# Stages by batch side by side, places in the same scope, and the second shared expert last

## The chip, the cores and the metric

The kernel runs on one core of one Trainium2 chip. Its time is the device time of one execution in microseconds (us). A core has a matrix engine (TensorE, PE in the profile; its weight loads are listed as PEld), a vector engine (VectorE, DVE), a scalar engine for activation functions and copies (ScalarE, ACT), a general engine (GpSimd, POOL) and one that mostly issues transfers (SyncE, SP). Each works through its own queue of instructions in order; between engines semaphores make one wait for another. Data lie in SBUF (128 partitions), products are formed in PSUM, and DMA queues move data to and from memory (HBM).

## What is computed

The reference takes `x` (4 batches of 512 rows of 512 numbers) through four layers, each an attention-like part and a feed-forward part, every part added to `x` with a gate. Cut to the parts that the change touches:

```python
# L1: attention weights from the context, applied to the rows of ln(x)
x = x + tanh(g_xattn[1]) * L1_xattn(layernorm(x), ctx, Wq, bq, Wk, bk)
# L1: one int8 linear layer, rows quantised one by one
x = x + tanh(g_ffn[1]) * L1_ffn(layernorm(x), weight, w_scale, bias)
# L2: a state-space model over ctx, gated by silu(layernorm(x))
x = x + tanh(g_xattn[2]) * L2_xattn(ctx, layernorm(x), ...)
# L2: 8 experts, the two best of each row, weights made to sum to 1
x = x + tanh(g_ffn[2]) * L2_ffn(layernorm(x), gate_w, w_gate, w_up, w_down)
# L3: attention with rotary positions over ctx
x = x + tanh(g_xattn[3]) * L3_xattn(layernorm(x), ctx, pos, pos, ...)
# L3: 2 shared experts for every row, and the two best of 16 for each row
x = x + tanh(g_ffn[3]) * L3_ffn(layernorm(x), Wsh_up, Wsh_down, Wrt_up, Wrt_down, W_router)
```

## The kernel before

`x` stays in SBUF for the whole kernel, as 16 tiles `x_0` to `x_15` of 128 rows; a batch `b` is four of them (`TB` is 4, `NB` is 4, `NT` is 16). Eight stages, `s0` to `s7`, stand for the eight lines of the reference (the four above that are not L0 are `s2`, `s3`, `s4`, `s5`, `s6`, `s7`). The program text gives the order of the instructions; a scheduler deals them to the engines' queues and may move one ahead inside a scope of higher priority. Tiles come from pools with a fixed number of buffers; a new tile waits until the buffer's last reader is done. A `with net.pools(...)` scope opens the pools of a stage; what comes behind it in the same memory waits for what was there.

Helpers that all stages use: `ln` (statistics on VectorE, L174 and L175; square root on ScalarE, L178; normalised rows `xl`, L205), `lnT` (the same, then 16 transposes on TensorE, L223, and four copies out of PSUM that `evict` deals in turn to VectorE, L162, and ScalarE, L161), `transposed` (four transposes, L234), `chain` (a sum of products on TensorE, L244), `residual` (adds a gated result to a tile of `x` on VectorE, L863).

- `s2`, per batch: two products `pq` with the context make q and k; then for each of four tiles of 128 rows: scores `pe` (L968), the row maximum on VectorE (L973), the exponential on ScalarE (L975), the scaling on VectorE (L977), a transpose into `aT`. Then `lnT` of the batch, four products `po` of four passes each, four residuals.
- `s3`, per batch: `ln`; the row's largest magnitude (L1003), two scalings and a cast on VectorE (L1011, L1014, L1016), a bf16 transpose (L1020), a product of four bf16 passes, then scale, bias and residual on VectorE (L1026, L1030, L863).
- `s4`, per batch: the state output `y` of the batch is loaded, `ln`, Silu on ScalarE (L1227), product with `y` on VectorE (L1229), transposes (L1233), residuals.
- `keys` makes the keys and values of `s6` from the context. It is a generator: `aside(n)` runs n parts of it at the place where it is called, in a scope with a small change of priority. A part has eight passes of `pkv`, the rotation of the keys on VectorE (L1562 to L1564), eight or so transposes (L1586) and two copies on ScalarE (L1655, L1672). In all there are 17 parts.
- `s5`: `top2` has the router (`lnT` of each batch, logits of all 16 tiles in one PSUM tile) and the choice of two experts a row; the normalised rows also go out to memory (`s_xs`) tile by tile. `places` sorts the rows by expert into 39 blocks of 128 rows: `ofi` (the expert of each block) early, the lists `to` and `from` last, behind a sum of 32 passes `inv`. `blocks` then runs over the 39 blocks: `up` reads the block's expert number on SP (`expert`, a value load) and has SP load that expert's weights (L1514 to L1519, 1.9 MB), the block's rows are gathered by an indirect transfer from POOL (L1428), and the results scattered by another (L1455). Results come back to `x` by `combine`: per tile a load `y2` of two times 128 rows and two residuals. `s5`'s results are combined inside `s6`, which isn't touched.
- `s7`: the same with 16 experts and 47 blocks (`rt` weights, 1 MB a block), and two shared experts (`sh0`, `sh1`) that run over all rows: per batch 16 passes `ph`, Gelu on ScalarE (L1990), 16 passes `po`, four residuals. The order in the text is router, places, shared expert 0, shared expert 1, blocks, combine with the write-out of `out` from ScalarE's queue.

The stages are called one after the other, each for all batches, from the driver at the end of the file. There the scopes are: `s2`, `s3`, `s4` and `keys` in one; `s5` whole in the next; `s6`; `s7`.

Of the kernel before, what the change touches and what calls it, by code (L numbers as in the profile page):

```python
# [19 lines left out]
P = 128  # L20
NB = 4
# [27 lines left out]
class Net:  # L49
# [893 lines left out]

    def s2(self, aside):
        nc, a = self.nc, self.a
        wqk = self.w("s2_w")[:, 0 : CC * 256].rearrange("p (c n) -> p c n", c=CC)
        nc.sync.dma_start(wqk, a["s2_w"].rearrange("(c p) n -> p c n", p=P))
        bqk = self.s("s2_b", 2)
        nc.sync.dma_start(bqk, a["s2_b"].rearrange("(k p) -> p k", p=P))
        for b in range(NB):  # L950
            qk = []
            cx = self.context("s2", b)
            for i in range(2):
                pq = self.mm(f"s2_pq_{b}_{i}")
                self.chain(
                    pq,
                    [
                        (wqk[:, c, i * P : (i + 1) * P], cx[:, c, :])
                        for c in range(CC)
                    ],  # L960
                )
                t = self.t(f"s2_qk_{b}_{i}")
                nc.vector.tensor_scalar(t, pq, bqk[:, i : i + 1], None, op0=ALU.add)
                qk.append(t)
            aT = self.w(f"s2_aT_{b}").rearrange("p (k n) -> p k n", k=TB)
            for m in range(TB):
                pe = self.mm(f"s2_pe_{b}_{m}")
                nc.tensor.matmul(  # L968
                    pe, lhsT=qk[0][:, m * P : (m + 1) * P], rhs=qk[1], start=True, stop=True
                )  # L970
                nmx = self.s(f"s2_nmx_{b}_{m}", 1, "s2_nmx")
                sm = self.s(f"s2_sm_{b}_{m}", 1, "s2_sm")
                nc.vector.tensor_reduce(nmx, pe, axis=AX.X, op=ALU.max, negate=True)  # L973
                at = self.t(f"s2_at_{b}_{m}")
                nc.scalar.activation(at, pe, AF.Exp, bias=nmx, accum_out=sm)  # L975
                nc.vector.reciprocal(sm, sm)
                nc.vector.tensor_scalar(at, at, sm, None, op0=ALU.mult)  # L977
# [11 lines left out]
    def s3(self, aside):  # L989
        nc, a = self.nc, self.a  # L990
# [6 lines left out]
        bias = self.bcast("s3_bias", a["s3_bias"])  # L997
        for b in range(NB):
            xl = self.ln(f"s3_{b}", self.x[b * TB : (b + 1) * TB])
            aside(1)  # L1000
            isc = self.s(f"s3_isc_{b}", TB, "s3_isc")
# [7 lines left out]
            for t in range(TB):  # L1009
# [20 lines left out]
                nc.vector.tensor_tensor(h, r, bias, op=ALU.add)  # L1030
                self.residual(b * TB + t, h, self.gf[:, 1:2])


# [182 lines left out]

    def s4(self, aside):
        nc = self.nc
        EC = DC
        for b in range(NB):  # L1220
            aside(1)
# [5 lines left out]
            nc.scalar.activation(g4, g4, AF.Silu)  # L1227
            for e in range(EC):
                nc.vector.tensor_tensor(g[:, e, :], g[:, e, :], y[:, e, :], op=ALU.mult)  # L1229
            for t in range(TB):  # L1230
                pt = self.mm(f"s4_pt_{b}_{t}")
                for e in range(EC):
                    nc.tensor.transpose(  # L1233
                        pt[:, e * P : (e + 1) * P], g[:, e, t * P : (t + 1) * P], self.ident
                    )
                self.residual(b * TB + t, pt, self.gx[:, 2:3])


    def top2(self, name, wr, E, keep=None):


        nc = self.nc
        pr = self.mm(f"{name}_pr")
        for b in range(NB):
            xT = self.lnT(f"{name}_{b}", b, rows=self.sorted[name][1])
            if keep is not None:
                keep.append(xT)
            for t in range(b * TB, (b + 1) * TB):
                self.chain(
                    pr[:, t * E : (t + 1) * E],  # L1250
                    [
                        (xT[:, c, (t % TB) * P : (t % TB + 1) * P], wr[:, c, :])
                        for c in range(DC)
                    ],
                )
        three = lambda v: v.rearrange("p (t e) -> p t e", e=E)
# [8 lines left out]
        m = row("m")  # L1265
        nc.vector.tensor_reduce(m, three(pr[:, 0 : NT * E]), axis=AX.X, op=ALU.max, negate=True)
        nc.vector.tensor_tensor(p, three(pr[:, 0 : NT * E]), wide(m), op=ALU.add)
        nc.scalar.activation(p, p, AF.Exp)
# [25 lines left out]

    def places(self, name, hots, E):

# [7 lines left out]
        tmp = lambda k, n: self.sp.tile([P, n], F32, tag=f"pl_{k}", name=f"{name}_{k}", bufs=1)  # L1304
        room = self.u(f"{name}_room")
        hot, keep, cnt, upto = (room[:, 256 * k : 256 * k + NT * E] for k in range(4))
# [37 lines left out]
        nc.vector.tensor_reduce(of, le, axis=AX.X, op=ALU.add)  # L1344
        ofi = self.sp.tile([P, blocks], I32, tag="pl_ofi", name=f"{name}_ofi", bufs=1)
        nc.vector.tensor_scalar(ofi, of, float(E - 1), None, op0=ALU.min)
# [27 lines left out]
        for i in range(2):  # L1374
# [42 lines left out]
        to, fr = (  # L1417
            self.sp.tile([P, blocks], I32, tag=f"pl_{k}", name=f"{name}_{k}", bufs=1)
            for k in ("to", "from")
        )  # L1420
# [69 lines left out]


    def s5(self):
        nc, a = self.nc, self.a
        E, I = 8, 352
        parts = [(0, P), (P, P), (2 * P, I - 2 * P)]
        wr = self.const.tile([P, DC, E], F32, name="s5_wr")
        nc.sync.dma_start(wr, a["s5_wr"].rearrange("(c p) e -> p c e", p=P))
        hots, tops, m, wide = self.top2("s5", wr, E)
        nc.vector.tensor_tensor(m, tops[0], tops[1], op=ALU.add)
        nc.vector.reciprocal(m, m)  # L1500
        for top in tops:
            nc.vector.tensor_tensor(top, top, m, op=ALU.mult)
        wt = self.gated("s5", hots, tops, m, self.gf[:, 2:3])
        places, ofi = self.places("s5", hots, E)

# [42 lines left out]
        self.blocks("s5", places, up, down)  # L1548
        self.wt5 = wt

# [409 lines left out]
    def s7(self, out):  # L1960
# [4 lines left out]
        xT = []  # L1965
        hots, tops, m, wide = self.top2("s7", wr, ERT, keep=xT)
        wt = self.gated("s7", hots, tops, m, self.gf[:, 3:4])
        places, ofi = self.places("s7", hots, ERT)

# [7 lines left out]

        for e in range(ESH):
            wu, wd = weights(f"sh{e}", a["s7_su"][e : e + 1], a["s7_sd"][e : e + 1])
            for b in range(NB):  # L1980
# [11 lines left out]
                for t in range(TB):  # L1992
                    po = self.mm(f"s7_po_{e}_{b}_{t}")
                    self.chain(
                        po, [(hT[i][:, t * P : (t + 1) * P], wd[:, i, :]) for i in range(2)]
                    )
                    self.residual(b * TB + t, po, self.gf[:, 3:4])

        def up(j, xb):
# [21 lines left out]
        self.blocks("s7", places, up, down)  # L2021
        self.combine("s7", wt, range(NT), out)


@with_exitstack
def kernel(ctx: ExitStack, tc: tile.TileContext, a: dict, out: bass.AP):
# [5 lines left out]
    with net.pools(cp=2, wp=8, up=2, bp=1, tp=8, sp=2, gp=1, qp=3, ps1=4, psb=1):  # L2032
# [10 lines left out]
        for _ in states:  # L2043
            pass
    with net.pools(cp=2, kp=1, rp=1, wp=8, bp=2, tp=10, sp=2, ps2=2, ps1=4):
        keys = net.keys()

        def aside(n):
            with tc.high_priority(offset=-400):
                for _ in range(n):  # L2050
                    next(keys, None)
# [12 lines left out]
    with net.pools(op=1, wp=6, bp=1, up=6, tp=8, sp=2, ps2=2, ps1=4):  # L2064
        net.s7(out)
# [83 lines left out]
```

## Time and profile before

| what | us |
|---|---|
| three runs, median (lowest to highest) | 3263.85 (3263.54 to 3266.96) |
| the profiled execution | 3266.79 |
| its span, first to last instruction | 3264.8 |
| TensorE busy in the span | 2816.4 (86%) |
| VectorE busy | 1953.6 (60%) |
| ScalarE busy | 1197.6 (37%) |
| mean granted TensorE clock | 0.922 of full speed |
| first product of `s2` to the last logit of `s5`'s router | 1450.4 to 1811.96 |
| last logit to the first product of `s5`'s blocks | 1811.96 to 1847.39 |
| shared expert 1 | 2980.2 to 3034.9 |
| blocks of `s7` | 3034.9 to 3226.2 |
| combine of `s7` | 3226.2 to 3264.8 |

A row of a table of stretches reads: the stretch, its length, then for PE, PEld, DVE, ACT and POOL the busy time with the number of instructions, the granted TensorE clock, the share of the 16 DMA engines that is busy, and what they move in GB/s. In the forty slices a digit is a busy share in tenths; in the chain of waits each line is a start, a length, an engine and the line of the kernel, each released by the one above. A transfer's line in a timeline shows when it is issued, not when it lands.

### The profile page before, as it was taken

Reading aid. Unit: us, or ns where it says so; the run is one execution under the profiler, and the core shown is the slowest. Engines: PE = TensorE matmul, PEld = TensorE weight load, DVE = VectorE, ACT = ScalarE, POOL = GpSimd, SP = SyncE. Lnnn points to the kernel's source line nnn. Section 1 sums busy time; section 2 is a strip of 40 time slices with the busy share of each in tenths; the row PEclk is TensorE's granted clock in tenths of the full one; section 3 lists DMA queues with packets and bytes.
Section 4 is the critical chain, followed back from the end, with each engine's and each line's share of the span. In section 5 each row is a group of like instructions: output and inputs, shape, how many; then the busy total and the mean of one; then the engine's idle time right before and its main releaser. Section 6 shows DMA issues by size and latency. Waiting matters only on the chain.

```text
span 3264.8 us, 43075 instructions
## 1 busy us (share of the span) xinstructions
PE 2816.4 (86%) x15772; PEld 1436.1 (44%) x15776; DVE 1953.6 (60%) x3212; ACT 1197.6 (37%) x2061; POOL 977.9 (30%) x939
## 2 busy tenths in 40 slices
PE   6899897878998898988836699977999999989994
PEld 2333332234444444444414588852333333254673
DVE  6565755477988879965687311138666666544103
ACT  2343442365554444433222111113555555520231
POOL 3465664435655646740000122210000000000351
PEclk8899998878999989999967699987999999989997
DMA  4000000266876768851212599972000000022798
GB/s 131 7 1 8 1 1 1 86 233 191 242 212 183 234 187 239 240 153 60 79 59 89 191 321 326 326 260 86 14 28 14 28 1 1 1 78 81 284 384 315
DMA packets 266898, 438.76 MB, mean 134 GB/s; under 512 B 32400, under 2 KB 114576, under 8 KB 265152
## 3 DMA queue, kind: packets, MB, share of 16 engines
q1 hardware_dynamic: 250624, 386.72, 37.0%
q0 software_dynamic: 13760, 45.10, 3.8%
q10 hardware_dynamic: 2304, 4.20, 0.3%
q8 instruction: 126, 2.06, 0.3%
q14 instruction: 84, 0.69, 0.1%
HBM read 370.79 MB, written 65.13 MB: 134 GB/s over the span
## 4 chain that ended last, share of the span: by engine, by line
PE 36%; DVE 8%; issue 4%; ACT 3%; POOL 2%; DMA 2%; POOLq 0%; DVEq 0%; ACTq 0%
PE s_po L244 9%; PE s_pl L268 8%; PE pg_s L244 6%; ACT pr_s L1939 2%; PE s_pq L244 2%; PE s_av L268 2%; PE s_ph L244 2%; POOL s_ys L1455 1%; DMA s_y<-s_ys 1%; DVE x L863 1%; POOL s_xb L1428 1%; PE s_pr L244 1%; PE s_pkv L244 1%; PE pt_s L223 1%; DVE st_s L174 1%
## 5 line engine op out<-in xcount | busy, mean ns | idle before, releaser
L1146 POOL TENSOR_TENSOR s_h<-s_h,s_C 128x512 f32<-128x512 f32 x256 | 449.2, 1754 | 292.1 <-DVE s_h L1145 249.8
L268 PE MATMUL s_pl<-s_qT,s_kT 32*128 32x512 f32 (+1 forms) x1536 | 447.4, 658 | 60.5 <-ACT pr_s L846 23.6
L268 PE MATMUL s_ps<-s_kT,s_qT 32*128 32x512 f32 (+1 forms) x1536 | 441.2, 677 | 12.7 <-DVE s_top L1819 5.9
L1819 DVE TENSOR_REDUCE s_top<-s_ps 128x1 f32<-128x512 f32 x512 | 328.5, 685 | 108.6 <-PE s_ps L268 108.4
L1939 ACT ACTIVATE pr_s<-s_pl 128x512 f32<-128x512 f32 x512 | 278.0, 595 | 307.2 <-PE s_ps L268 297.5
L1145 DVE TENSOR_TENSOR_SCAN s_h<-s_da,s_db 128x512 f32<-128x512 f32 x256 | 312.1, 1219 | 62.6 <-PE s_y L268 36.1
L1144 ACT ACTIVATE s_da<-s_rdl,s_A 128x512 f32<-128x512 f32 x256 | 184.4, 722 | 331.5 <-DVE s_h L1145 329.4
L268 PE MATMUL s_av<-pr_s,s_v 128*32 128x256 f32 (+1 forms) x3072 | 250.8, 398 | 0.2
L244 PE MATMUL s_ph<-xT_s,s_wu 128*128 128x256 f32 x1024 | 246.4, 395 | 0.7 <-ACT xT_s L161 0.7
L905 PE MATMUL s_acc<-s_wd,s_hT 128*128 128x512 f32 x512 | 239.9, 612 | 5.7 <-ACT s_hT L936 5.7
L244 PEld LDWEIGHTS s_ph<-xT_s,s_wu 128*128 128x128 f32 x1024 | 197.3, 197 | 77.9 <-issue 49.7
L244 PEld LDWEIGHTS pg_s<-s_xbT,s_w 128*128 128x128 f32 (+1 forms) x1872 | 213.9, 183 | 19.8 <-issue 17.8
L268 PEld LDWEIGHTS s_pl<-s_qT,s_kT 32*128 32x128 f32 (+1 forms) x1536 | 118.4, 186 | 226.8 <-ACT pr_s L1939 95.9
L244 PE MATMUL pg_s<-s_xbT,s_w 128*128 128x128 f32 (+1 forms) x1872 | 215.5, 275 | 1.4 <-ACT s_xbT L161 1.4
L694 DVE TENSOR_REDUCE s_nmx<-s_ps 128x1 f32<-128x496 f32 x256 | 158.4, 662 | 91.8 <-PE s_ps L268 81.0
L1143 DVE TENSOR_TENSOR s_db<-s_B,s_rdu 128x512 f32<-128x512 f32 x256 | 203.6, 795 | 12.7 <-DMA s_B<-s_bc 5.0
L1332 POOL IOTA s_js<- 128x39 f32 (+1 forms) x2 | 0.4, 178 | 686.8 <-DVE x L863 686.8
L1428 POOL DMA_INDIRECT s_xb<-s_xs,s_from x86 | 83.5, 971 | 380.0 <-PE ptr_s_xb L234 235.2
L846 ACT ACTIVATE pr_s<-s_pl 128x512 f32<-128x512 f32 (+1 forms) x256 | 138.8, 594 | 158.6 <-PE s_pl L268 83.8
L268 PE MATMUL s_y<-s_h,ident 64*64 64x512 f32 x1024 | 146.8, 637 | 53.1 <-issue 28.6
L268 PEld LDWEIGHTS s_av<-pr_s,s_v 128*32 128x32 f32 (+1 forms) x3072 | 61.4, 109 | 285.7 <-issue 253.6
L1534 DVE TENSOR_TENSOR g_s<-g_s,pg_s 128x256 f32<-128x256 f32 x78 | 27.5, 352 | 264.2 <-ACT g_s L1533 264.2
(388 smaller groups left out, 4453.8 us busy)
## 6 DMA issues: line engine op xcount, KB each, us to landing
s_B<-s_bc SPq DMA_DIRECT2D x256, 256.0 KB, 5.0
s_C<-s_bc SPq DMA_DIRECT2D x256, 256.0 KB, 4.4
s_w<-in_s_wg SPq DMA_DIRECT2D x39, 704.0 KB, 4.7
s_w<-in_s_wu SPq DMA_DIRECT2D x39, 704.0 KB, 6.7
s_w_rt<-in_s_ru SPq DMA_DIRECT2D x47, 512.0 KB, 10.8
s_w_rt<-in_s_rd SPq DMA_DIRECT2D x47, 512.0 KB, 12.1
s_w<-in_s_wd SPq DMA_DIRECT2D x39, 512.0 KB, 8.2
s_y<-s_ys SPq DMA_DIRECT2D x32, 512.0 KB, 5.7
```

The source lines that it names most:

```text
L244: ins = self.nc.tensor.matmul(out, lhsT=l, rhs=r, start=(i == 0), stop=(i == len(pairs) - 1)).ins
L268: ins = self.nc.tensor.matmul(out, lhsT=l, rhs=r, **flags).ins
L694: ins = nc.vector.tensor_reduce(nmx[:, at + i : at + i + 1], ps[i][0][:, 0:M], axis=AX.X, op=ALU.max, negate=True,).ins
L846: ins = nc.scalar.activation(prs[i][0:n, j, :], pl[j][0][0:n, :], AF.Exp).ins
L905: ins = nc.tensor.matmul(accs[i][t], lhsT=hT[:, j, t * P : (t + 1) * P], rhs=wd[f // 4][:, f % 4, :], start=(f == 0), stop=(f == FC - 1),).ins
L1143: nc.vector.tensor_tensor(db, br, du, op=ALU.mult)
L1144: nc.scalar.activation(da, dl, AF.Exp, scale=am[:, e, n : n + 1])
L1145: nc.vector.tensor_tensor_scan(h, da, db, 0.0, op0=ALU.mult, op1=ALU.add)
L1146: nc.gpsimd.tensor_tensor(h, h, cr, op=ALU.mult)
L1428: self.nc.gpsimd.indirect_dma_start(out=t, out_offset=None, in_=self.sorted[name][1], in_offset=bass.IndirectOffsetOnAxis(ap=fr[:, j : j + ...
L1819: ins = nc.vector.tensor_reduce(dst[:, i], ps[i][0], axis=AX.X, op=ALU.max, negate=True).ins
L1939: ins = nc.scalar.activation(prs[i][:, j, :], pl[j][0], AF.Exp).ins
```

## The change

`s2`, `s3` and `s4` no longer loop over the batches; each loads its weights and returns `batch(b)`, a generator that stops (`yield`) at places inside the batch: in `s2` after q and k, after every second tile, after `lnT` and after every second product; in `s3` after the norm and after each tile; in `s4` after the Silu and after every second tile. The router is taken out of `top2` and returned the same way, with one PSUM tile per batch, from which ScalarE copies the logits to an SBUF tile `lg`. The driver runs seven steps; in a step, batch `step - i` of stage i is run for each of the four stages, one piece of each in turn, and every second turn one part of `keys`. The scope takes one pool more (`op`, from `places`) and 12 instead of 10 buffers for `t`. `s5_places` (`top2` and `places`) follows in the same scope, its working tile from the pool `w` instead of `u`; `lg`, `ofi`, `to` and `from` lie in an outer pool `hp`. The blocks of `s5` get a scope of their own. In `s7` shared expert 1 is run behind the blocks, batch by batch, with the combine of the batch before it after each; y2 has 6 buffers instead of 4.

```diff
-    def s2(self, aside):
+    def s2(self):
...
-        for b in range(NB):
+        def batch(b):
...
                 qk.append(t)
+            yield
...
                 self.transposed(f"s2_{b}_{m}", at, aT[:, :, m * P : (m + 1) * P], m)
+                if m % 2:
+                    yield
             xT = self.lnT(f"s2_{b}", b, room=self.w)
-            aside(2)
+            yield
             for t in range(TB):
...
                 self.residual(b * TB + t, po, self.gx[:, 1:2])
+                if t % 2:
+                    yield
+        return batch
...
-    def top2(self, name, wr, E, keep=None):
+    def router(self, name, wr, E, room=None, keep=None):
+        lg = self.hp.tile([P, NT * E], F32, name=f"{name}_lg")
+        def batch(b):
+            xT = self.lnT(f"{name}_{b}", b, rows=self.sorted[name][1], room=room)
             if keep is not None:
                 keep.append(xT)
+            yield
+            pr = self.mm(f"{name}_pr_{b}")[:, 0 : TB * E]
+            for t in range(TB):
                 self.chain(
                     pr[:, t * E : (t + 1) * E],
+                    [(xT[:, c, t * P : (t + 1) * P], wr[:, c, :]) for c in range(DC)],
+                )
+            self.nc.scalar.copy(lg[:, b * TB * E : (b + 1) * TB * E], pr)
+        return lg, batch
...
+    def s5_places(self):
+        nc = self.nc
+        hots, tops, m, wide = self.top2("s5", self.lg5, 8)
...
+        self.wt5 = self.gated("s5", hots, tops, m, self.gf[:, 2:3])
+        self.places5 = self.places("s5", hots, 8, self.w)
...
-        for e in range(ESH):
+        def shared(e):
...
+                yield
+        for e in range(ESH - 1):
+            for _ in shared(e):
+                pass
...
         self.blocks("s7", places, up, down)
-        self.combine("s7", wt, range(NT), out)
+        done = lambda b: self.combine("s7", wt, range(b * TB, (b + 1) * TB), out)
+        for b, _ in enumerate(shared(ESH - 1)):
+            if b:
+                done(b - 1)
+        done(NB - 1)
...
-        net.s2(aside)
-        net.s3(aside)
-        net.s4(aside)
-        for _ in keys:
-            pass
+    with net.pools(hp=1):
+        with net.pools(op=1, cp=2, kp=1, rp=1, wp=8, bp=2, tp=12, sp=2, ps2=2, ps1=4):
...
+            stages = [net.s2(), net.s3(), net.s4(), net.s5_router()]
+            turns = 0
+            for step in range(NB + len(stages) - 1):
+                going = [f(step - i) for i, f in enumerate(stages) if 0 <= step - i < NB]
+                while going:
+                    going = [g for g in going if next(g, going) is None]
+                    turns += 1
+                    if turns % 2:
+                        aside(1)
+            for _ in keys:
+                pass
+            net.s5_places()
+        with net.pools(ep=4, bp=1, tp=8, ps2=2, ps1=4):
+            net.s5()
     net.y2 = 2
-    with net.pools(op=1, ep=4, bp=1, up=3, tp=8, sp=2, ps2=2, ps1=4):
-        net.s5()
...
-    net.y2 = 4
-    with net.pools(op=1, wp=6, bp=1, up=6, tp=8, sp=2, ps2=2, ps1=4):
+    net.y2 = 6
+    with net.pools(hp=1, op=1, wp=6, bp=1, up=6, tp=8, sp=2, ps2=2, ps1=4):
         net.s7(out)
```

More of the change, by code (lines that the diff above doesn't have):

```diff
@@ L986, in s2, with s3 @@
                 self.residual(b * TB + t, po, self.gx[:, 1:2])
-    def s3(self, aside):
+                if t % 2:
+                    yield
+        return batch
+    def s3(self):
         nc, a = self.nc, self.a
@@ L997, in s3 @@
         bias = self.bcast("s3_bias", a["s3_bias"])
-        for b in range(NB):
+        def batch(b):
             xl = self.ln(f"s3_{b}", self.x[b * TB : (b + 1) * TB])
-            aside(1)
+            yield
             isc = self.s(f"s3_isc_{b}", TB, "s3_isc")
@@ L1031, in s3 @@
                 self.residual(b * TB + t, h, self.gf[:, 1:2])
+                yield
+        return batch
     def states(self):
@@ L1215, in states, with s4, batch @@
         channels_done(*done)()
-    def s4(self, aside):
+    def s4(self):
         nc = self.nc
         EC = DC
-        for b in range(NB):
-            aside(1)
+        def batch(b):
             y = self.w(f"s4_y4_{b}").rearrange("p (c n) -> p c n", c=EC)
@@ L1227, in s4 @@
             nc.scalar.activation(g4, g4, AF.Silu)
+            yield
             for e in range(EC):
@@ L1236, in s4, with batch, top2 @@
                 self.residual(b * TB + t, pt, self.gx[:, 2:3])
-    def top2(self, name, wr, E, keep=None):
[L1242 to L1245, printed above, removed]
+                if t % 2:
+                    yield
+        return batch
+    def router(self, name, wr, E, room=None, keep=None):
+        lg = self.hp.tile([P, NT * E], F32, name=f"{name}_lg")
+        def batch(b):
+            xT = self.lnT(f"{name}_{b}", b, rows=self.sorted[name][1], room=room)
             if keep is not None:
                 keep.append(xT)
-            for t in range(b * TB, (b + 1) * TB):
+            yield
+            pr = self.mm(f"{name}_pr_{b}")[:, 0 : TB * E]
+            for t in range(TB):
                 self.chain(
                     pr[:, t * E : (t + 1) * E],
[L1251 to L1254, printed above, removed]
-                )
+                    [(xT[:, c, t * P : (t + 1) * P], wr[:, c, :]) for c in range(DC)],
+                )
+            self.nc.scalar.copy(lg[:, b * TB * E : (b + 1) * TB * E], pr)
+        return lg, batch
+    def top2(self, name, lg, E):
+        nc = self.nc
         three = lambda v: v.rearrange("p (t e) -> p t e", e=E)
@@ L1265, in top2 @@
         m = row("m")
-        nc.vector.tensor_reduce(m, three(pr[:, 0 : NT * E]), axis=AX.X, op=ALU.max, negate=True)
-        nc.vector.tensor_tensor(p, three(pr[:, 0 : NT * E]), wide(m), op=ALU.add)
+        nc.vector.tensor_reduce(m, three(lg), axis=AX.X, op=ALU.max, negate=True)
+        nc.vector.tensor_tensor(p, three(lg), wide(m), op=ALU.add)
         nc.scalar.activation(p, p, AF.Exp)
@@ L1292, in gated, with places @@
         return tops
-    def places(self, name, hots, E):
+    def places(self, name, hots, E, room):
         nc = self.nc
@@ L1304, in places @@
         tmp = lambda k, n: self.sp.tile([P, n], F32, tag=f"pl_{k}", name=f"{name}_{k}", bufs=1)
-        room = self.u(f"{name}_room")
+        room = room(f"{name}_room")
         hot, keep, cnt, upto = (room[:, 256 * k : 256 * k + NT * E] for k in range(4))
@@ L1344, in places @@
         nc.vector.tensor_reduce(of, le, axis=AX.X, op=ALU.add)
-        ofi = self.sp.tile([P, blocks], I32, tag="pl_ofi", name=f"{name}_ofi", bufs=1)
+        ofi = self.hp.tile([P, blocks], I32, name=f"{name}_ofi")
         nc.vector.tensor_scalar(ofi, of, float(E - 1), None, op0=ALU.min)
@@ L1417, in places @@
         to, fr = (
-            self.sp.tile([P, blocks], I32, tag=f"pl_{k}", name=f"{name}_{k}", bufs=1)
-            for k in ("to", "from")
+            self.hp.tile([P, blocks], I32, name=f"{name}_{k}") for k in ("to", "from")
         )
@@ L1489, in combine, with s5_router @@
                 self.nc.scalar.dma_start(out[t * P : (t + 1) * P, :], self.x[t])
+    def s5_router(self):
+        wr = self.const.tile([P, DC, 8], F32, name="s5_wr")
+        self.nc.sync.dma_start(wr, self.a["s5_wr"].rearrange("(c p) e -> p c e", p=P))
+        self.lg5, batch = self.router("s5", wr, 8, self.w)
+        return batch
+    def s5_places(self):
+        nc = self.nc
+        hots, tops, m, wide = self.top2("s5", self.lg5, 8)
+        nc.vector.tensor_tensor(m, tops[0], tops[1], op=ALU.add)
+        nc.vector.reciprocal(m, m)
+        for top in tops:
+            nc.vector.tensor_tensor(top, top, m, op=ALU.mult)
+        self.wt5 = self.gated("s5", hots, tops, m, self.gf[:, 2:3])
+        self.places5 = self.places("s5", hots, 8, self.w)
     def s5(self):
@@ L1495, in s5 @@
         parts = [(0, P), (P, P), (2 * P, I - 2 * P)]
[L1496 to L1504, printed above, removed]
+        places, ofi = self.places5
         def up(j, xT):
@@ L1548, in s5 @@
         self.blocks("s5", places, up, down)
-        self.wt5 = wt
     def rope(self, name, ps, t, out):
@@ L1965, in s7 @@
         xT = []
-        hots, tops, m, wide = self.top2("s7", wr, ERT, keep=xT)
+        lg, batch = self.router("s7", wr, ERT, keep=xT)
+        for b in range(NB):
+            for _ in batch(b):
+                pass
+        hots, tops, m, wide = self.top2("s7", lg, ERT)
         wt = self.gated("s7", hots, tops, m, self.gf[:, 3:4])
-        places, ofi = self.places("s7", hots, ERT)
+        places, ofi = self.places("s7", hots, ERT, self.u)
         def weights(name, up, dn):
@@ L1997, in s7 @@
                     self.residual(b * TB + t, po, self.gf[:, 3:4])
+                yield
+        for e in range(ESH - 1):
+            for _ in shared(e):
+                pass
         def up(j, xb):
@@ L2044, with aside @@
             pass
[L2045 to L2051, printed above, removed]
-        net.s2(aside)
-        net.s3(aside)
-        net.s4(aside)
-        for _ in keys:
-            pass
+    with net.pools(hp=1):
+        with net.pools(op=1, cp=2, kp=1, rp=1, wp=8, bp=2, tp=12, sp=2, ps2=2, ps1=4):
+            keys = net.keys()
+            def aside(n):
+                with tc.high_priority(offset=-400):
+                    for _ in range(n):
+                        next(keys, None)
+            stages = [net.s2(), net.s3(), net.s4(), net.s5_router()]
[8 more added lines that the diff above has]
+            for _ in keys:
+                pass
+            net.s5_places()
+        with net.pools(ep=4, bp=1, tp=8, ps2=2, ps1=4):
+            net.s5()
     net.y2 = 2
-    with net.pools(op=1, ep=4, bp=1, up=3, tp=8, sp=2, ps2=2, ps1=4):
-        net.s5()
     with net.pools(wp=2, kq=4, vp=2, up=1, rp=1, tp=8, bp=1, sp=2, ps3=4, ps1=1):
         net.s6()
-    net.y2 = 4
-    with net.pools(op=1, wp=6, bp=1, up=6, tp=8, sp=2, ps2=2, ps1=4):
+    net.y2 = 6
+    with net.pools(hp=1, op=1, wp=6, bp=1, up=6, tp=8, sp=2, ps2=2, ps1=4):
         net.s7(out)
```

## The prediction

> **What bounds the kernel now.** I read the forty slices first, for where the stages lie and who is full in them; then the chain of waits, for what each stage waits for; then busy time by stretch, whose rows are the terms of the sum; then groups by shape, for single durations. The slices (82 us each):
>
> ```profile
> PE   6899897878998898988836699977999999989994
> DVE  6565755477988879965687311138666666544103
> PEclk8899998878999989999967699987999999989997
> DMA  4000000266876768851212599972000000022798
> ```
>
> The change touches slices 18 to 22 (TensorE falls to 3, 6, 6; its clock to 6 and 7) and the last four. The stretches, with the times between which I take each stage:
>
> ```profile
> core 0: us, PE busy (x) PEld busy (x) DVE busy (x) ACT busy (x) POOL busy (x), PEclk, DMA share, GB/s
> 1492.60:1530.70 38.10, 33.66 (x114) 17.04 (x113) 20.94 (x47) 11.44 (x19) 0.00 (x0) 1.00 0.21 70
> ...
> 1667.30:1704.60 37.30, 13.46 (x47) 6.16 (x48) 34.66 (x83) 12.33 (x12) 0.00 (x0) 0.60 0.16 51
> ...
> 1776.60:1811.96 35.36, 33.69 (x192) 32.04 (x190) 15.93 (x38) 7.49 (x12) 0.32 (x2) 0.63 0.43 155
> 1811.96:1847.39 35.43, 5.80 (x41) 4.74 (x41) 20.12 (x60) 0.93 (x3) 5.38 (x6) 0.50 0.68 230
> 2980.20:3034.90 54.70, 53.95 (x127) 23.18 (x126) 12.01 (x16) 4.34 (x8) 0.00 (x0) 1.00 0.06 19
> 3034.90:3226.20 191.30, 185.97 (x1129) 139.87 (x1126) 17.36 (x25) 58.77 (x117) 87.22 (x89) 1.00 0.98 353
> 3226.20:3264.80 38.60, 0.00 (x0) 0.00 (x0) 23.79 (x32) 0.00 (x0) 0.00 (x0) 0.50 0.89 326
> ```
>
> These rows are one s2 batch (TensorE-bound), one s3 batch (VectorE 34.66 of 37.30, TensorE a third), s5's router, s5's places, and at the end shared expert 1, the 47 blocks and the combine. Shared expert 1 has TensorE full and the DMA queues at 0.06; the combine has TensorE at nothing and the queues at 0.89. The chain shows what an s2 tile hangs on:
>
> ```profile
> 1507.19 0.88 PE s_pe L968 x2
> 1508.09 0.70 DVE s_nmx L973
> 1508.81 0.79 ACT s_at L975 x2
> 1509.82 0.50 DVE s_at L977
> 1510.36 0.66 PE ptr_s L234 x4
> ```
>
> It passes from TensorE to VectorE, ScalarE, VectorE and back, 3.5 to 4 us a tile, with nothing else in the four queues. Whoever puts other work into them lengthens it.
>
> **The tail (s7).** Shared expert 1 is moved from before the blocks to behind them. All its instructions go along, in the emitted order: TensorE runs shared expert 0, 47 blocks, then shared expert 1; its products are not mixed into the blocks. So the blocks begin 54.7 us earlier, and their last product, which ended at 3222.4, ends at 3167.7. Behind it stand four batches of 16 and 16 passes, 6.87 + 7.02 = 13.9 by the chain's rows, 55.6, plus 0.9 for the last Gelu, which nothing follows: 3224.2. The combine's 16 loads of 512 KB (38.6 us with the write-out) now run below those 56 us: the queues carried 19 GB/s there, and loading is behind the last scatter (2.7 us) just as before. VectorE has four residuals and eight combine steps a batch, 12 x 0.75 = 9, below TensorE's 13.9. After the last product three VectorE steps (2.3) and the write-out (3.75 between the last VectorE step, 3261.05, and the end) remain: end 3230.3 instead of 3264.8, **34 won**. Queues passed: SP now issues five routed experts' loads ahead instead of four, and shared expert 1's only when block 41 frees its buffer, some 20 us before they are needed; ScalarE issues the write-outs ahead of the next Gelu, with y2 buffers raised from 4 to 6. Bounds: 28, if every write-out holds the next batch's Gelu by 2 us; 36.
>
> **s2 to the router.** Before, 1450.4 to 1811.96, 361.6 us. By batch, summed from the groups' mean durations at full clock (TensorE, VectorE): s2 24.9 and 16.4; s3 6.6 and 21; s4 3.5 and 9.6; router 8.4 and 6; one of 17 parts of the keys 4.3 and 2.25. After, step 0 is s2 alone, step 1 s2 and s3, step 2 with s4, step 3 all four, steps 4 to 6 run out; keys fall at 3.5 parts a step, gone by step 4. The larger engine per step is then 42 (as the first batch took), 46.5 (TensorE), 55, 61, 43 (VectorE), and 25 and 14 for the last two, where one batch hangs on its own chain: 287. That is the lower bound, 75 won.
>
> What it leaves out: the in-order queues. I followed the emitted order with single durations. In step 1, an s2 tile's maximum, exponential and scaling stand between s3's quantising steps: 59. In step 2 the first exponential stands on ScalarE behind the square roots and the Silu of s3's and s4's norms, which themselves wait for VectorE: it comes 24 us into the step instead of 6, TensorE is empty from 12 to 25, and the step takes 70. In step 3 the fourth batch's q and k are evicted by VectorE behind s4's and the router's norms (16.4), its first scores come at 21: 83. Steps 4 to 6: s3's last batch, its own chain with s4's and the router's work between, 56; then 25 and 14. Sum 42 + 59 + 70 + 83 + 95 = 349. Not in it: the low clock in the holes and waits for PSUM and tile buffers. The same four products of s3 took 1.05 at clock 1.0 and 1.90 in the 0.6 stretches; the steps have three holes of about 12 and the last two run thin: 8. Buffers (four PSUM tiles for four stages, 12 tile buffers that s5's row writes free only on landing): 3. **360, 2 won**. Worst: 380 to 386, if each of 12 exponentials in steps 1 to 3 waits 2 us beyond this.
>
> On the clock the row is: 0.60 with TensorE at 13.46 of 37.30, 1.00 at 33.66 of 38.10. The Trainium skill, "TensorE: Matmul & The Clock Gate", Part 1, says that half rate follows an idle window of about 3.4 us and full rate a busy one of as long. By that, three holes of 12 us cost an estimated 3 x 1.7 = 5 for the rewarming; the sum would be 3 lower. The rule speaks against a stretch that is interleaved but has holes, and the trace agrees in direction.
>
> **Between router and blocks.** Before, logits end 1811.96, the first block's product starts 1847.39. Router logits are now copied from PSUM by ScalarE: one 128x32 copy on the path, 0.35 (512 columns take 0.59); in s7 0.5, half hidden by shared expert 0. Blocks now have pools of their own, opened behind the places' pools: in the order of SP's queue 31 reads of the block's expert number stand ahead of the first weight load, before one. Price of one:
>
> ```profile
> 1824.98 0.62 SPq L1519 DMA_DIRECT2D s_w<-in_s_wd  x1
> 1826.40 0.38 SPq L1514 DMA_DIRECT2D s_w<-in_s_wg  x1
> ```
>
> Between these two lie a read and a gap: 0.80; the gap between loads of one expert is 0.19, so 0.61 a read. 31 take 18.9 behind ofi (10.2 after the logits): the first load is issued at 29 after the logits, before at 11.3. It takes about 7 to land, and the rows of the first block, fetched through POOL behind inv, arrive at 34 and gate the first product as before. Only the later loads are late: three buffers filled by 1847 before; now 1.92 MB a block at 325 GB/s, 5.9, against 8.33 TensorE needs a block. Loss 3; bounds 0 and 10. At the stretch's head s6_wkv is loaded behind s1's last product, up to 1; s2_w gates there anyway.
>
> **Sum.** 3264.8 - 34 - 2 + 3 + 0.6 = 3232.4 as a span. The profiled execution took 3266.8 as a whole, 2.0 above its span and 2.9 above the median of 3263.85; 3232.4 + 2.0 - 2.9 = 3231.5, and I say **3230**.
>
> **Rivals.** (B) The stretch overlaps nearly as the busy times allow: the waits I put at 62 above 287 fall to 20 to 30. For it: VectorE holds 245 of 361.6, TensorE 254, much of it at low clock, the router's 33.69 at 0.63. Against: s2's chain through all four queues. 3231 - 45 = 3186 (3165 to 3212). (C) Slower: ScalarE's queue holds s2's exponentials behind other stages' roots, Silus and 1.28 us table loads, tile for tile: 12 tiles in steps 1 to 3 at 4 to 6 us beyond my walk, 48 to 72, with the clock low throughout; the 34 is eaten from about 2.9 us a tile on: 3272. Against: half of those tiles come after the norms of their step. (D) The combine isn't hidden: write-outs in ScalarE's queue or y2 buffers let it run behind the shared expert; 38.6 stays, 3265. Against: queues at 0.06 below it. (E) The interleave does nothing, since the scheduler keeps stage order; the emitted order speaks against it, and it would give 3231 too.
>
> **Chances.** Forecast 0.54 (3214 to 3250), B 0.29, C 0.10, D 0.04, the rest 0.03. About 0.2%, 6.5 us, is what can be told from no change. Range 3174 to 3256: it holds the forecast and most of B. Faster: forecast, B and part of the rest, 0.85; same 0.05; slower 0.10.
>
> **What would show it.** TensorE full and y2 loads landing in the last 56 us, end some 6 us behind the last product: the tail. The time from the first pq to the last logit: 360, else B (below 335) or C (above 395); in step 2 a hole of about 12 before the second scores, released by ScalarE. The first wg issue 29 after the last logit and blocks 8.33 apart from the fourth on. I am wrong if the stretch differs by more than 15, or if the weights' late start costs more than the rows' arrival hides.

## The result and the profile after

| | us |
|---|---|
| before, median (lowest to highest) | 3263.69 (3261.83 to 3266.96), four runs |
| changed, median (lowest to highest) | 3212.78 (3208.02 to 3218.71), four runs |
| ratio, with its 95% interval | 0.9844 (0.9822 to 0.9865) |
| predicted | 3230 (3174 to 3256) |
| the profiled execution of the changed kernel and its span | 3208.97, 3207.3 |

The changed kernel is 51 us faster. The forecast was 34; the difference lies in one stretch. The forty slices of the changed kernel, 80 us each:

```profile
PE   6899898768988989998776599987999999989999
DVE  6665666378897979976777411118666666735004
PEclk8899999878999989999897699997999999989999
DMA  4000000177676767862222499964000000013996
```

From slice 19 on TensorE reads 8, 7, 7, 6, 5 where it read 8, 8, 3, 6, 6; at the end it reads 9 to the last slice where it ended in a 4, and the DMA queues end in 3, 9, 9, 6 where they ended in 2, 7, 9, 8. The stretches, in the columns of the table of before:

```profile
core 0: us, PE busy (x) PEld busy (x) DVE busy (x) ACT busy (x) POOL busy (x), PEclk, DMA share, GB/s
1447.31:1786.03 338.72, 252.46 (x958) 144.34 (x958) 247.91 (x570) 93.22 (x140) 0.84 (x3) 0.85 0.23 75
1786.03:1821.12 35.09, 5.77 (x40) 4.75 (x41) 20.12 (x60) 3.65 (x5) 6.38 (x7) 0.50 0.16 52
1821.12:2149.35 328.23, 327.55 (x2258) 270.88 (x2258) 40.62 (x97) 55.29 (x135) 69.69 (x72) 0.99 0.94 314
2962.50:3143.95 181.45, 180.94 (x1087) 135.35 (x1086) 15.92 (x23) 56.97 (x114) 84.20 (x86) 1.00 1.02 367
3143.95:3207.30 63.35, 55.49 (x129) 23.64 (x127) 34.24 (x49) 4.34 (x8) 1.13 (x2) 0.98 0.61 207
```

The rows are: first product of `s2` to the last logit; from there to the first product of the blocks; the 39 blocks; the 47 blocks of `s7`; from their last product to the end. The first of them, in the profile of the kernel before, was:

```profile
1450.43:1811.94 361.51, 253.89 (x948) 145.87 (x952) 244.83 (x567) 93.08 (x137) 0.32 (x2) 0.81 0.21 71
```

Busy times are the same within 3.1 us (TensorE 253.89 and 252.46, VectorE 244.83 and 247.91); the length fell by 22.8. Nothing was made cheaper; TensorE's idle time went from 107.6 to 86.3.

With both profiles cut at the same events, the 57.5 us between the two spans come out like this (changed less before, us, each time rounded):

| stretch | before | changed | difference |
|---|---|---|---|
| start to `s1`'s last product (code untouched) | 1443.8 | 1439.9 | -3.9 |
| to `s2`'s first product | 6.7 | 7.4 | +0.8 |
| to the router's last logit | 361.5 | 338.7 | -22.8 |
| to the first product of `s5`'s blocks | 35.5 | 35.1 | -0.4 |
| 39 blocks | 327.4 | 328.2 | +0.8 |
| to the first `pb` product of `s7`'s blocks | 866.9 | 813.1 | -53.8 |
| 47 blocks | 180.8 | 181.4 | +0.6 |
| to the end | 42.4 | 63.3 | +20.9 |

The first row is chance: over the twelve profiles of this study `s1` ended between 1434.2 and 1444.3, with the same instructions of TensorE, VectorE and ScalarE ahead of it; E4 below, the changed kernel once more, has the 1434.2.

### The profile page after: what moved, and what is told of

It is laid out like the page before. It is cut to its first block, busy times and chain, and to the rows that moved or that the text cites. A ratio compares the mean times of both kernels' runs of the same rounds, so it can differ in the third digit from the quotient of the medians.

```text
span 3207.3 us, 43093 instructions
## 1 busy us (share of the span) xinstructions
PE 2814.8 (88%) x15776; PEld 1434.8 (45%) x15776; DVE 1952.4 (61%) x3212; ACT 1200.9 (37%) x2071; POOL 976.3 (30%) x939
## 5 line engine op out<-in xcount | busy, mean ns | idle before, releaser
L1157 ACT ACTIVATE s_da<-s_rdl,s_A 128x512 f32<-128x512 f32 x256 | 184.4, 722 | 328.2 <-DVE s_h L1158 324.7
```

The costliest lines, as they stand in the source:

```text
L1157: nc.scalar.activation(da, dl, AF.Exp, scale=am[:, e, n : n + 1])
```

## The experiments

**The parts alone.** E1 to E4 ran side by side on one chip. E1 is the kernel before with the order of `s7` changed and nothing else:

```diff
-        for e in range(ESH):
+        for e in range(ESH - 1):
+            for _ in shared(e):
+                pass
...
-        self.combine("s7", wt, range(NT), out)
+        done = lambda b: self.combine("s7", wt, range(b * TB, (b + 1) * TB), out)
+        for b, _ in enumerate(shared(ESH - 1)):
+            if b:
+                done(b - 1)
+        done(NB - 1)
...
-    net.y2 = 4
+    net.y2 = 6
```

Expected:

> The kernel before with shared expert 1 and the combine moved behind s7's blocks, nothing else. Theory (the tail is worth the 54.7 us of the shared expert less about 21 us that the end grows by): 34 us faster, 3228 to 3232, and the end comes 62 to 63 us after the last block's product. Rival (the tail is worth more, and the stretch little): 45 us or more, below 3220. Rival (the write-outs or the y2 loads hold the shared expert): under 28 us, above 3236.

Measured: 3228.01 against 3261.45 (ratio 0.9897, 0.988 to 0.9913), 33.4 us faster, and the end comes 63.0 us after the last block's product. The theory holds, its rivals fall.

E2 is the changed kernel with `s7` as it was (the diff above, undone):

> The changed kernel with s7 in its old order (shared expert 1 before the blocks, combine alone at the end, 4 buffers for y2). Theory (the interleaved stretch takes 339 us instead of 361.6): 17 to 23 us faster than the kernel before, 3241 to 3247. Rival (the stretch is even, as forecast, and the rest of the difference in the profile is chance of one execution): 3258 to 3264.

Measured: 3252.52 (3239.44 to 3259.16, ten runs), 8.9 us faster (ratio 0.9971, 0.9957 to 0.9984). Neither expectation. In its profile the stretch is 344.3, 17 below the 361.5 of the first profile of before, but it is only 12 below E1's 356.1, where the stretch has before's code; and from `s5`'s last product to `s6`'s first it took 30.2 us instead of 26.7. So the expectation rested on one profile of before that was a long one, and something behind the blocks takes part of the gain back; E7 finds it.

E3 keeps the changed kernel's scopes, pools and tail, and runs the batches stage by stage:

```diff
-            for step in range(NB + len(stages) - 1):
-                going = [f(step - i) for i, f in enumerate(stages) if 0 <= step - i < NB]
-                while going:
...
+            for i, f in enumerate(stages):
+                for b in range(NB):
+                    if i == 2:
+                        aside(1)
...
+                    for k, _ in enumerate(f(b)):
+                        if i == 0 and k == 3:
+                            aside(2)
+                        if i == 1 and k == 0:
+                            aside(1)
```

> The changed kernel with its scopes, pools and tail, but the batches run stage by stage and the keys at the places of before. Theory (the interleave itself makes the gain of the stretch): the stretch from the first pq to the last logit goes back to 358 to 364 us and the time to 3228 to 3236. Rival (the new pools make it: 12 tile buffers, places in the same scope, the router's room): within 5 us of the changed kernel, 3208 to 3218.

Measured: 3232.18 (3229.05 to 3233.32; ratio 0.9913, 0.9896 to 0.9929). Its stretch:

```profile
1443.84:1800.93 357.09, 250.91 (x958) 141.45 (x958) 246.15 (x570) 93.44 (x140) 0.84 (x3) 0.82 0.22 71
```

357.09 us with the same 251 of TensorE and 246 of VectorE: the interleave makes the gain, not the pools.

E4 is the changed kernel again:

> The changed kernel once more, for a second profile and for its spread (3208 to 3219 over four runs). Theory (the spread comes from the TensorE clock in the stretch, which has holes): a time near 3217 goes with a stretch near 348 and a lower granted clock there, one near 3208 with 339. Rival (it comes from s0 and s1, whose end lay 3.9 us apart between the two profiles): the stretch is 339 in both, and the difference lies ahead of it.

Measured: 3214.82 (3210.28 to 3220.84; ratio 0.9863, 0.9842 to 0.9884), the profiled execution 3211.58, with `s1` ending at 1434.2 and a stretch of 342.9. Both theories say too little: against the first profile the stretch is 4.2 longer and `s1` 5.7 shorter. No execution near 3217 was profiled, so what makes those stays open; one source is shown below.

These four give the parts from medians of runs taken together: the tail -33.4 (E1 against before), the new scopes +4.2 (E3 against E1), the interleave -17.4 (E4 against E3); together -46.6, which is E4 against before. Scopes and interleave are -13.2 in this sum and -8.9 in E2, which has them without the new tail; the ten runs of E2 lie 20 us apart, and what spreads them stays open.

**Where the interleave loses.** The changed kernel, per step, against the walk of the prediction (steps 4 to 6, behind `s2`'s last product, are called the drain; it is cut at `s3`'s last product):

| | step 0 | 1 | 2 | 3 | `s3`'s last batch | rest | sum |
|---|---|---|---|---|---|---|---|
| walked | 42 | 59 | 70 | 83 | 56 | 39 | 349 |
| changed | 42.2 | 60.0 | 71.2 | 77.2 | 52.7 | 35.3 | 338.7 |
| E2 | 41.9 | 60.3 | 71.3 | 82.9 | 52.9 | 35.1 | 344.3 |
| E4 | 42.6 | 61.2 | 71.2 | 79.8 | 52.8 | 35.3 | 342.9 |

Step 2 has the hole that was walked, 9.2 us instead of 12 to 13. ScalarE's queue and TensorE's in the changed kernel (start, duration, engine, line, operation, and in brackets what the engine waited for):

```profile
1557.21 0.30 ACT L178 ACTIVATE rs_s<-mv_s,eps 128x4 f32<-128x4 f32 x1 [2.84 <-DVE mv_s L175]
...
1560.93 1.91 ACT L1240 ACTIVATE s_g<-s_g 128x2048 f32<-128x2048 f32 x1
...
1569.12 0.30 ACT L178 ACTIVATE rs_s<-mv_s,eps 128x4 f32<-128x4 f32 x1 [4.98 <-DVE mv_s L175]
1569.44 1.28 ACT L978 ACT_TABLE_LOAD   x1
1570.73 0.69 ACT L978 ACTIVATE s_at<-s_pe,s_nmx 128x512 f32<-128x512 f32 x1
```

```profile
1559.67 3.70 PE L244 MATMUL s_pkv<-s_wkv,ctx_s 128*128 128x512 f32 x8 [1.17 <-ACT s_kt L1703]
1572.57 0.47 PE L1617 MATMUL pt_s6k<-ident,s_k_r 128*128 128x128 f32 x1 [9.20 <-ACT s_vs L1686]
1572.96 1.11 PE L234 MATMUL ptr_s<-ident,s_at 128*128 128x128 f32 x4
```

The first exponential of the step (L978) starts at 1570.73, 21.2 us into it, behind the square roots of the other stages' norms (L178) and the Silu (L1240); TensorE ends its products of the keys at 1563.4 and stands for 9.2 us. The releaser is named as a copy of the keys (`s_vs`), which ScalarE ran right behind that exponential: one queue holds both. E5 lets `s2` run ahead in each step:

```diff
                 going = [f(step - i) for i, f in enumerate(stages) if 0 <= step - i < NB]
+                if step < NB:
+                    next(going[0])
+                    next(going[0])
                 while going:
```

> The changed kernel, where in each of the first four steps s2's batch runs its first two pieces (q and k, two tiles) before the other stages begin. Theory (the holes of steps 2 and 3 come from s2's exponentials standing in ScalarE's queue behind the other stages' square roots and Silu): the hole of 9.2 us in step 2 and most of three holes of 3.4 to 4.6 in step 3 go, steps 2 and 3 shrink from 71 and 80 to about 62 and 72, the stretch from 342 to about 325, the time to 3197 to 3203. Rival (VectorE's work in its queue is what limits; putting s2 first makes the other stages late by as much): the stretch stays at 336 to 348.

Measured: 3218.59 (3211.94 to 3222.35; ratio 0.9879, 0.9861 to 0.9896), no gain, and the stretch is 339.7, as the rival has it. But the steps were 48.8, 66.4, 69.0, 64.9 and then 90.5: steps 2 and 3 shrank, as the theory has it, and steps 0 and 1 together grew by 11 to 13 us. So E9 has the lead in steps 2 and 3 alone, on the kernel of E7 below:

```diff
+                if step in (2, 3):
+                    next(going[0])
+                    next(going[0])
```

> The kernel of the pool kept open for s6, where s2's batch runs its first two pieces ahead of the other stages in steps 2 and 3 only. With the lead in all four steps, steps 2 and 3 took 69.0 and 64.9 instead of 71.2 and 77 to 83, and steps 0 and 1 48.8 and 66.4 instead of 42 and 60. Theory (a lead helps where the exponentials stood behind the square roots and the Silu of s4 and the router, which begin in steps 2 and 3, and harms where s2 has only its own chain and the keys to fill it): steps 42, 60, 69, 65, then 90; the stretch 326, the time 3196 to 3203. Rival (what the lead wins in steps 2 and 3 is work that steps 0 and 1 had done earlier, VectorE's above all): steps 2 and 3 come back to 145 or more in sum, the stretch 338 to 344.

Measured: 3199.77 (3199.26 to 3201.87; ratio 0.9805, 0.9789 to 0.9821). Its steps, the last three in one row:

```profile
1451.91:1493.90 41.99, 37.59 (x110) 19.03 (x111) 26.52 (x68) 12.68 (x22) 0.00 (x0) 0.95 0.20 62
1493.90:1552.90 59.00, 48.94 (x181) 24.66 (x182) 45.51 (x104) 15.81 (x26) 0.00 (x0) 1.00 0.23 72
1552.90:1616.40 63.50, 49.83 (x175) 26.27 (x176) 52.42 (x120) 24.00 (x32) 0.00 (x0) 0.84 0.22 68
1616.40:1685.46 69.06, 50.62 (x197) 30.18 (x198) 52.73 (x119) 22.30 (x32) 0.00 (x0) 0.83 0.27 85
1685.46:1780.73 95.27, 60.01 (x295) 42.14 (x293) 69.94 (x159) 23.42 (x32) 0.32 (x2) 0.73 0.26 87
```

42.0, 59.0, 63.5, 69.1, 95.3: the sum is 328.8 where 326 was expected; steps 2 and 3 lost 18 us against E4 (71.2 and 79.8), and the drain took 7 back (95.3 against 88.1). The edit also moves work: the two pieces ahead count no turns, so 16 products of the keys (two parts) leave step 3 for the drain, and one part's work on VectorE leaves step 2. The net gain is what counts, 9.7 us of the stretch against E7 (338.5) and 14.1 against E4. In ScalarE's queue the exponentials (L978) now stand between the roots and the Silu:

```profile
1556.02 0.30 ACT L178 ACTIVATE rs_s<-mv_s,eps 128x4 f32<-128x4 f32 x1 [3.23 <-DVE mv_s L175]
...
1560.64 0.69 ACT L978 ACTIVATE s_at<-s_pe,s_nmx 128x512 f32<-128x512 f32 x1
...
1562.73 0.30 ACT L178 ACTIVATE rs_s<-mv_s,eps 128x4 f32<-128x4 f32 x1
...
1565.25 0.69 ACT L978 ACTIVATE s_at<-s_pe,s_nmx 128x512 f32<-128x512 f32 x1
...
1567.35 1.91 ACT L1240 ACTIVATE s_g<-s_g 128x2048 f32<-128x2048 f32 x1
```

The first starts at 1560.64, 7.7 us into the step. Four table loads of 1.28 us more are paid for it in this step, and still it is 7.7 us shorter, with as many products of the keys in it (24) as in the changed kernel. The queue's order held the exponentials, not ScalarE's load; how much of step 3's gain is the order and how much the moved keys, no run separates. This kernel beats both: it is 64 us under before, where the changed kernel is 47 to 51 under and E7 48 (each against runs of before beside it; E9 and E10 ran on another chip than E1 to E8).

E10 gives the lead to step 4 too, where `s3`'s last batch comes first:

> The same with the lead in step 4 too, where s3's last batch is the first in turn. Theory (the drain hangs on s3's last batch; let ahead of s4 and the router it ends earlier): steps 4 to 6 from 88 to 90 down to 82, 6 to 8 us faster than with the lead in steps 2 and 3. Rival (VectorE does the work of all three in any order, and the last router batch waits for the same sum): no change within 3 us.

Measured: 3201.73 (3198.88 to 3205.12; ratio 0.9815, 0.9798 to 0.9831); the drain 94.3 against 95.3. The rival holds: no change.

E6 takes the keys out of step 0 (`if turns % 2 and step:`):

> The changed kernel, where no part of the keys runs in step 0; the parts that it had there run in steps 4 and 5. Theory (the last three steps, 88 us with TensorE idle for over a third, have room; step 0 is TensorE-bound with keys): step 0 from 42 to about 34, steps 4 to 6 from 88 to about 90, the stretch 336. Rival (step 0 is bound by the chain of its tiles, and the keys lie in its gaps): step 0 stays at 39 to 42, and steps 4 to 6 grow by VectorE's 2.25 us a part, 7 to 9 in sum: slower, 349.

Measured: 3223.23 (3218.98 to 3225.14; ratio 0.9885, 0.9867 to 0.9903), by the median slower than E4, though the intervals overlap. Step 0 and the drain:

```profile
1451.52:1493.60 42.08, 36.05 (x96) 17.50 (x97) 18.33 (x36) 8.32 (x15) 0.00 (x0) 0.90 0.09 29
1700.09:1794.56 94.47, 66.26 (x295) 45.57 (x294) 66.80 (x157) 25.64 (x34) 0.32 (x2) 0.76 0.28 93
```

The edit did half of what it says: 16 products of the keys (22 in the changed kernel) still moved ahead into step 0, so that TensorE's share of the theory was hardly tested, and what left it is their work on VectorE, 8 us (18.33 against 26.52 in E9's row). Step 0 takes 42.08 all the same: that work cost nothing there. The drain grew from 88.1 to 94.5, and a part of the keys now runs behind the last logit, so that the first product of the blocks comes 38.3 us after it instead of 35.1. In this the rival holds; the whole stretch, 343.0, is as long as E4's, where 349 was expected.

**Between the stages.** E8 puts `s5_places` back into the scope of the blocks, so that one read of an expert number, not 31, stands ahead of the first weight load:

```diff
-            net.s5_places()
-        with net.pools(ep=4, bp=1, tp=8, ps2=2, ps1=4):
+        with net.pools(op=1, ep=4, bp=1, up=1, tp=8, sp=2, ps2=2, ps1=4):
+            net.s5_places()
             net.s5()
```

> The changed kernel, where s5_places stands in the scope of the blocks as before, so that one read of an expert number instead of 31 stands ahead of the first weight load on SP. Theory (the rows of the first block gate it, and the late weights cost only what the first product waits for them, 3.1 us in the profile, less what the blocks lose later, 0.8): first weight load about 12 us after the last logit instead of 29, first product 34 to 35 us after it as before, 39 blocks in 327.4 instead of 328.3: 0 to 2 us faster. Rival (the rows are late too, because the weights share the queues with them): first product up to 5 us earlier, or later.

Measured: 3212.8 (3205.42 to 3220.16; ratio 0.985, 0.9831 to 0.9868). The first weight load on SP's queue in the changed kernel (last logit 1786.03), then in E8 (last logit 1791.87):

```profile
1815.48 0.43 SPq L1546 DMA_DIRECT2D s_w<-in_s_wg  x1
```

```profile
1803.98 0.42 SPq L1546 DMA_DIRECT2D s_w<-in_s_wg  x1
```

29.4 us after the logits there, 12.1 here; the first product stands 35.1 and 35.9 after them, and the 39 blocks take 328.2 and 328.7. What the first product (`pg`, behind the transposes `ptr_s_xb` of the block's rows) waits for is not the same in the two. The changed kernel, then E8:

```profile
1816.90 1.09 PE L234 MATMUL ptr_s_xb<-ident,s_xb 128*128 128x128 f32 x4 [5.67 <-DMA s_xb<-s_xs,s_from]
1821.12 7.98 PE L244 MATMUL pg_s<-s_xbT,s_w 128*128 128x128 f32 x48 [3.14 <-DMA s_w<-in_s_wg]
```

```profile
1825.94 1.12 PE L234 MATMUL ptr_s_xb<-ident,s_xb 128*128 128x128 f32 x4 [8.98 <-DMA s_xb<-s_xs,s_from]
1827.79 8.49 PE L244 MATMUL pg_s<-s_xbT,s_w 128*128 128x128 f32 x48 [0.73 <-ACT s_xbT L161]
```

In the changed kernel the rows are there 30.9 us after the logits, and the product waits 3.14 more for the late weights; in E8 the weights are there first, and the rows come at 34.1, though POOL issued their transfer at the same point (27.2 and 27.1). The queues were 0.16 busy between the logits and this product in the changed kernel, 0.66 in E8, which fits the rival's reason, rows and weights in the same queues. So 17 us of the weights' issue were worth nothing: the rows lost by it what the weights gained.

E7 keeps the pool of `to` and `from` open until `s6` is done:

```diff
-    net.y2 = 2
-    with net.pools(wp=2, kq=4, vp=2, up=1, rp=1, tp=8, bp=1, sp=2, ps3=4, ps1=1):
-        net.s6()
+        net.y2 = 2
+        with net.pools(wp=2, kq=4, vp=2, up=1, rp=1, tp=8, bp=1, sp=2, ps3=4, ps1=1):
+            net.s6()
```

> The changed kernel, where the pool that holds to, from, ofi and lg stays open until s6 is done, so that s6's first weights do not lie where these are. Theory (the 28 to 31 us from s5's last product to s6's first, against 26.7 before, come from wq, which waits for the last scatters that read to): wq is issued some 10 us before the last block ends, as before, and the time to s6's first product is 26.5 to 27: 1.5 to 4 us faster. Rival (it comes from the combine's loads, which the change did not touch): 28 to 31 again.

Measured: 3211.43 (3208.08 to 3213.39; ratio 0.9855, 0.9837 to 0.9873). SP's queue behind the blocks in the changed kernel (last product of the blocks 2149.4), and in E7 (2151.2):

```profile
2153.34 0.38 SPq L1711 DMA_DIRECT2D s_wq<-in_s_wq  x1
2153.77 1.01 SPq L1508 DMA_DIRECT2D s_y<-s_ys  x2
```

```profile
2140.75 0.38 SPq L1711 DMA_DIRECT2D s_wq<-in_s_wq  x1
2141.18 0.52 SPq L1930 DMA_DIRECT2D s_wo<-in_s_wo  x1
2154.93 0.88 SPq L1508 DMA_DIRECT2D s_y<-s_ys  x2
```

`wq` went out 4 us behind the last block and next to the combine's first loads; with the pool kept open, it goes out 10 us ahead of the end. `s5`'s last product to `s6`'s first takes 26.8 instead of 28.1 and 30.7, as before the change (26.7). Over all profiles it takes 25.0 to 26.9 where the pool is kept (E7, E9, E10) and 28.1 to 30.7 where it is not (the changed kernel, E2 to E6, E8). That the pool's end holds `wq` is shown; which of its four tiles does it was not tested, and in the medians the 1.3 to 4 us are within the spread.

## The prediction by its own steps

**The tail** was right in size and cause: 34 forecast, 33.4 measured (E1), 33.8 between the profiles (54.7 won, 20.9 of it given back). The end of the chain of waits in the changed kernel:

```profile
3186.30 6.02 PE s_ph L244 x14
...
3192.34 0.61 ACT s_h L2026
...
3192.99 2.00 PE s_po L244 x4
...
3195.02 0.76 DVE x L863
...
3202.80 0.75 DVE x L863
```

TensorE goes on from batch to batch; the only wait is the 0.6 for the last Gelu. In the last batch the chain passes to VectorE behind the first product; TensorE's last product ends at 3200.13, VectorE's last step 3.4 us later (2.3 were summed), and the write-out takes 3.7 more. From the last block's product to the last product of the shared expert it was 56.2, where 56.5 was summed. The combine's loads lay below it: the queues 0.61 busy over the whole tail, against 0.89 before.

**The stretch** was right in sign, and its size is the step that failed: 2 forecast, 17 measured (E4 against E3). By the prediction's own sign of being wrong, a stretch more than 15 from 360, it was wrong here: 338.7, 342.9 and 344.3. The walk of the queues was near, 349, with steps 0 to 2 within 2.2 us each; it was long in step 3 and in the drain (88 measured, 95 walked). What took it away from the measurement is the 11 us put on top, 8 for the low clock and 3 for buffers. The low clock was there, and it was waited for: granted 0.65 in the drain, three of `s3`'s last four products took 1.89, and VectorE stood 9.0 us for one of them, which was held in TensorE's queue by 32 products of the router. These took 6.83, and 3.64 in step 3:

```profile
1725.73 6.83 PE L244 MATMUL s_pr<-s_wr,xT_s 128*128 128x8 f32 x32
```

```profile
1737.93 0.75 DVE L1036 SCALAR_TENSOR_TENSOR s_r<-s_po,s_isc,s_wsc 128x512 f32<-128x512 f32 x1 [8.98 <-PE s_po L244]
```

And still the drain was 7 us under the walk: over all steps the walk, at full clock, was 5 to 10 us longer than what came with slow products in it. Which waits it counted that did not come stays open, and no run here measures the 8 or the 3 by itself. The other part of the miss is the row the sum was made against: 361.5 in that profile, 356.1 and 357.1 in the two others with the old order, so that a part of the -22.8 of the profiles is chance.

**The Trainium skill's rule on the clock gate** was weighed as 5 us for three holes, against 8 from rows. TensorE's busy time in the stretch was 252.46 and 255.78 in the two profiles of the changed kernel, and 253.89, 248.79 (E1) and 250.91 (E3) with the old order: the holes cost at most a few us more rewarming than those they replaced. Which of the two figures is nearer no run shows.

**Reads and weights**: first load 29 after the logits forecast, 29.4 measured; the 3 us of loss for the blocks were 0.8, with -0.4 ahead of them, and E8 shows nothing to win. The total was right and the gate was not: the rows were to arrive at 34 and gate the first product as before, and they arrived at 30.9 and the weights gated it.

**The copies of the logits** take 0.20 each, 0.35 was forecast. **The stage's start**: 0.8 of "up to 1".

**Not foreseen**: +1.4 to +4 at the start of `s6`. The prediction followed the pools into the blocks and not out of them: by E7, something in the pool that now lives to the last scatter lay where `s6`'s first weights go.

**The rivals.** The median, 3212.8, lies just below the forecast's own range (3214 to 3250), at the edge of B's (3165 to 3212). What B describes needed the lead of E9, and there the stretch, 328.8, still lies 42 above the sum of the larger engines, 287. C (slower, ScalarE's queue beyond the walk) fell: the wait was there, at about the size walked; C's price of 3272 also did not follow from its own 48 to 72 us, which on 3231 give 3279 and more. D fell with E1. E fell with E3 against E4.

## What to carry to other kernels

Side by side in program order is not yet side by side in the queues: look at which stage's first instruction stands in front of another's chain in each in-order queue, and let the stage with the long chain begin first only where others would stand in front of it. When a sum has been walked through the queues, take what is put on top of it from a wait that a row shows: here 11 us were added to a walk that was 5 to 10 us long already. When a transfer is moved, ask what else is in the queues at that time: in E8 the weights came early and the rows late. When a scope is split, ask of every tile that outlives it what comes to lie in its place next.

## What the runs showed of the hardware

The same instructions, in the same order and with TensorE busy throughout, took different times because the clock was granted differently. At `s7`'s router and shared expert 0, the changed kernel and E7 run the same sequence (second and third part of it in each; columns as above, the clock third from the end):

```profile
2872.04:2877.70 5.66, 5.66 (x24) 4.63 (x24) 3.25 (x8) 1.68 (x4) 0.00 (x0) 0.52 0.01 3
2877.70:2887.68 9.98, 9.98 (x39) 6.30 (x39) 3.40 (x10) 0.21 (x1) 0.00 (x0) 0.66 0.28 105
```

```profile
2873.27:2876.28 3.01, 3.01 (x25) 2.53 (x24) 1.68 (x4) 1.29 (x3) 0.00 (x0) 1.00 0.16 59
2876.28:2882.92 6.64, 6.64 (x39) 4.68 (x38) 4.96 (x14) 0.51 (x2) 0.00 (x0) 1.00 0.43 160
```

5.66 and 9.98 us at 0.52 and 0.66 in one, 3.01 and 6.64 at 1.00 in the other; the whole passage from the first logit product to the last took 36.7 and 29.8. TensorE is full in all four rows, so a full queue alone didn't raise the clock here; many of these products move 16 columns. The Trainium skill, "TensorE: Matmul & The Clock Gate", Part 1, speaks of full rate after one busy window of about 3.4 us; 5.66 us of back-to-back work at 0.52, behind 8.77 us in which TensorE was busy without a break, do not agree with it, if a busy window is one that the profile calls busy. The clock was granted and taken back within this work: in the changed kernel two products of 512 columns took 1.10 us at 2867.39, 1.92 at 2875.49 and 1.10 at 2877.70. Slow ones stand behind runs of the 16-column products (in E7 1.98 at 2889.02, behind 32 of them), though not behind every run; whether these products are the reason no run here tests. The clock moved 7 us in code that both kernels have alike, and the runs of the changed kernel spread over 13 us.
